# Two small matmuls of zeros in every 64th iteration of a three-layer convolution kernel

## The chip, the cores and the metric

The kernel runs on one core of a Trainium2 chip. The metric is the device time of one execution in microseconds (us). Of three runs of the kernel before, the median is 2720.43 us, the lowest 2719.11 and the highest 2721.21.

## The reference

The input `x` has the shape (4, 32, 32, 16): four batches, 32 x 32 pixels, 16 channels. Three layers of one form follow each other, and a fourth of another form. Cut to what matters:

```python
# layers 0, 1, 2, with x group-normalised first; the result is added to x
first   = einsum('ijpq,bpqc->bijc', M, x)
shifted = conv(x, G)                       # 3x3, 'SAME', for every output pixel (i,j) its own kernel
diff    = relu(x[:, :, :, None, None, :] - shifted)
second  = einsum('ijpq,bpqijc->bijc', W, diff)
x       = x + first - second
# layer 3: a rational 2-d filter, by Fourier transforms
```

The weight of the work is `second`: for each of 1024 output pixels (i,j) there is a 3x3 convolution of the whole image with kernels of its own, a relu, and a weighted sum over all 1024 input pixels.

## The kernel before

**The main loop.** One iteration takes one block `blk` (eight output pixels by 16 channels: 128 output partitions) and one batch `b`. There are 3 layers x 128 blocks x 4 batches = 1536 iterations. The list `order` holds them, and `now["at"]` is the number of the present one. Within an iteration TensorE (PE) fills a pair of PSUM banks `pt` [128, 2, 512] with x minus the convolution, and VectorE (DVE) reduces it with one instruction, L764: the minimum with 0, times the weight tile `w`, summed along the row.

**Two halves of the rows.** The contraction is only 64 long. So nearly every matmul uses 64 of the array's 128 rows: it is issued twice, first for partitions 0 to 63 (below: the upper half) into bank 0 of the pair, then for partitions 64 to 127 (the lower half) into bank 1. In the trace such an instruction has the tile form `64*128`: 64 rows by 128 columns. The two halves hold different data and write different banks, so nothing in the program ties one to the other.

**What an iteration issues.** The first 24 iterations go through `direct` (L699). All the others, 1512, go through `shared_products` and `own_products`:

- `shared_products(i + 1)`, L718: 3 matmuls for each half, 256 columns, in float32r (one pass), for the *next* iteration; ScalarE (ACT) then copies the result to the other half of the columns (L727).
- `own_products(i)`, L749: for each half two float32 matmuls of 256 columns, each of which the hardware does in two passes, so 4 passes; then two float32r matmuls of 512 columns.

So each half executes 9 weight loads and 9 matmul passes an iteration: 3 at L718, 4 at L749 with the tile `f`, and 2 at L749 with the tiles `n` and `g`. ACT clears part of a pair ahead of time (L681), and `prepare` gives out the four pairs in turn.

**What sets the order.** The order is written by hand (`manual_schedule`); the rest of the work is cut into generators that `step()` advances once an iteration: loads of `w`, `f` and `g`, GpSimd's preparation of taps, group norm (matmuls at L167 and L174, with `avg_r` as weights and zeros or statistics as moving data), the first term (`first_term`, L495, three times: 16 float32 matmuls of the form `128*64`, all 128 rows by 64 columns, in two passes each), and at the end layer 3 (L887, L927, L1067).

**Names in the change.** `avg_r` is a float32r constant [128, 128], `nought_r` is a [128, 2] tile of zeros, and `pt` is the pair that `own_products` accumulates into.

Of the kernel before, what the change touches and what calls it, by code (L numbers as in the profile page):

```python
# [15 lines left out]
P = 128  # L16
# [23 lines left out]
def conv_stack_kernel(ctx, tc, x, M, W, raw_f, first_g, F, E, h0, coef, cst, dft, idp, idq, out):  # L40
    nc = tc.nc
# [17 lines left out]
    def pair_psum(stays_full=False):  # L59
        slot = banks[0] % 4  # L60
        banks[0] += 1
        if not stays_full:
            full[slot] = False
        return ps.tile([P, 2, 512], F32, tag=f"pt{slot}", name="pt")
# [19 lines left out]
    avg_r = const.tile([P, P], F32R, name="avg_r")  # L84
# [4 lines left out]
    nought_r = const.tile([P, 2], F32R, name="nought_r")  # L89
# [14 lines left out]
    start = [[range(layer * NBLK + lo, layer * NBLK + hi) for lo, hi in spans[layer]] for layer in range(3)]  # L104
# [20 lines left out]
    now = {"at": 0}  # L125
# [470 lines left out]
    def taps_of(u, blk, half, dys, slot=1):  # L596
        rows = slice(64 * half, 64 * half + 64)
        if u < 3:
            return first_gt[u][rows, bass.ts(blk % GC, P)]
        v, blk = divmod(blk % GC, 2)  # L600
        return gt[uses[u][0]][rows, dys[half], v, slot, bass.ts(blk, P)]
# [7 lines left out]
    for q in qs:  # L609
        load = max(0, done[-2] + 5, ready[q] - 20)  # L610
        at = load, max(ready[q], done[-1] + 1, load + (6 if q else 3))
# [51 lines left out]
    def prepare(i, rearm=False):  # L663

        if i in pts or i >= len(order):
            return
        slot = banks[0] % 4
        if is_shared(i) and not full[slot] and not rearm and is_shared(now["at"]) and i == now["at"] + 2:
            return
        pts[i] = pt = pair_psum(True)  # L670
        if is_shared(i):
            if not full[slot]:
                blk, b, _ = order[now["at"]]
                ni = ims[blk // NBLK, b][1].rearrange("p y k m -> p (y k m)")
                for half in range(2):
                    rows = slice(64 * half, 64 * half + 64)
                    nc.tensor.matmul(
                        pt[:, half], lhsT=avg_r[rows], rhs=ni[rows, :512], start=True, stop=True
                    )
            here = by_pixel(pt)[:, :, 0]  # L680
            nc.scalar.copy(here, nought.unsqueeze(2).to_broadcast(list(here.shape)))  # L681
        full[slot] = True
# [4 lines left out]
    def of_half(pt, half, k):  # L687
        return pt[:, half].rearrange("p (l k x) -> p l k x", k=2, x=64)[:, :, k]
# [40 lines left out]
    def own_products(u, blk, b, pt):  # L729


        f = fours[uses[u][0]]
        at = bass.ts(blk % GC, P)
        fi, ni = ims[blk // NBLK, b]
        products = [lambda half, rows, k=k: (of_half(pt, half, k), f[rows, k, at], fi[rows, :, k]) for k in range(2)]
        for dys in ((0, 2), (2, 0)):
            products.append(
                lambda half, rows, dys=dys: (
                    pt[:, half],
                    taps_of(u, blk, half, dys),  # L740
                    ni[rows, dys[half] : dys[half] + 4, :2].rearrange("p l k m -> p l (k m)"),
                )
            )
        for n, operands in enumerate(products):
            if n == 2:
                prepare(now["at"] + 2, True)
            for half in range(2):
                to, w, rhs = operands(half, slice(64 * half, 64 * half + 64))
                nc.tensor.matmul(to, lhsT=w, rhs=rhs, start=False, stop=n == 3, skip_group_check=True)  # L749
# [434 lines left out]
    pt = pair_psum()  # L1184
# [175 lines left out]
```

## Time and profile before

| | value |
|---|---|
| median of 3 runs | 2720.43 us |
| the profiled execution's own time | 2729.58 us |
| its span, first to last instruction | 2727.8 us |
| PE busy | 2695.6 us (99%) |
| DVE busy | 1944.3 us (71%) |
| ACT busy | 1777.8 us (65%) |
| GpSimd busy | 845.6 us (31%) |
| mean granted TensorE clock | 0.997 |
| DMA | 652.93 MB, 239 GB/s |

The profiled execution is 9.2 us slower than the median of the runs, and 1.8 us of it lie around the span. "Busy" counts the time from an instruction's recorded start to its modelled end; matmuls overlap, so a busy PE may still lose time between two of them. A weight load (PEld) of the next matmul runs beside the present matmul. In this trace it begins about 2 ns after the present matmul's columns begin to stream, so that the starts of the weight loads tell when each pass really began.

### The profile page before, as it was taken

The page shows a single profiled execution, that of the slowest core. Times are in us where ns is not written, and L with a number is a line of the kernel's source. Part 1 is how long each engine was busy: PE and PEld are TensorE (multiplying, and loading weights), DVE is VectorE, ACT ScalarE, POOL GpSimd, SP SyncE. Part 2 cuts the span into 40 slices and gives each one's busy share as a digit, 9 for nine tenths or more (in the row PEclk, how much of TensorE's full clock was granted, in tenths as well). Part 3 has the DMA queues.
Part 4 walks back from the last instruction along what each step waited for, and adds up shares of the span by engine and source line. Part 5 has one row for each costly group of instructions (what it writes and reads, how often), then busy time and mean ns, then how long its engine had stood idle before and what let it go on. Part 6 is the DMA issues. An engine that isn't in the chain of part 4 may idle for free.

```text
span 2727.8 us, 69513 instructions
## 1 busy us (share of the span) xinstructions
PE 2695.6 (99%) x28402; PEld 2525.1 (93%) x28402; DVE 1944.3 (71%) x3246; ACT 1777.8 (65%) x3114; POOL 845.6 (31%) x1164
## 2 busy tenths in 40 slices
PE   7999999999999999999999999999999999999999
PEld 4899988888888899999999999989999999999995
DVE  6676876777777777677777777777767777777773
ACT  2566666666666676666666666666666666666661
POOL 5534354422312342322222221234332322232011
PEclk9999999999999999999999999999999999999999
DMA  8896567576664987565566657497866756676525
GB/s 298 300 343 235 185 229 273 203 264 221 254 257 182 315 258 292 211 244 225 223 231 239 246 219 282 179 326 240 316 210 225 265 218 254 228 249 241 224 84 84
DMA packets 134703, 652.93 MB, mean 239 GB/s; under 512 B 16992, under 2 KB 27376, under 8 KB 95344
## 3 DMA queue, kind: packets, MB, share of 16 engines
q1 hardware_dynamic: 85472, 475.99, 47.2%
q0 software_dynamic: 48480, 171.85, 19.6%
q8 instruction: 223, 3.65, 0.6%
q14 instruction: 96, 0.79, 0.1%
q10 hardware_dynamic: 432, 0.66, 0.1%
HBM read 488.81 MB, written 159.61 MB: 238 GB/s over the span
## 4 chain that ended last, share of the span: by engine, by line
PE 84%; DMA 1%; DVE 0%; POOL 0%; ACT 0%; issue 0%; SPq 0%; DVEq 0%; POOLq 0%
PE pt L749 67%; PE pt L718 14%; PE pt L1067 2%; DMA n<-img 1%; PE pt L495 1%; DMA g<-gd 0%; DMA img<-ye 0%; DVE junk L764 0%; ACT pt L681 0%; PE pt L887 0%; POOL ys L414 0%; POOL ys L421 0%; PE pt L167 0%; SPq L461 0%; PE pt L927 0%
## 5 line engine op out<-in xcount | busy, mean ns | idle before, releaser
L764 DVE SCALAR_TENSOR_TENSOR junk<-pt,w 128x1024 f32<-128x1024 f32 x1536 | 1881.0, 1225 | 736.0 <-PE pt L749 693.7
L749 PE MATMUL pt<-f,f 64*128 64x256 f32 x12096 | 1692.5, 377 | 0.0
L749 PE MATMUL pt<-n,g 64*128 64x512 f32 x6048 | 1354.5, 483 | 0.0
L749 PEld LDWEIGHTS pt<-f,f 64*128 64x128 f32 x12096 | 1212.3, 186 | 24.3
L681 ACT COPY pt<-nought_r 128x512 f32<-128x512 f32 x1512 | 888.7, 588 | 497.7 <-DVE junk L764 495.2
L727 ACT COPY pt<-pt 128x512 f32<-128x512 f32 x1512 | 860.7, 569 | 292.5 <-PE pt L718 291.7
L718 PEld LDWEIGHTS pt<-n,g 64*128 64x128 f32 x9072 | 919.2, 185 | 74.4 <-ACT pt L681 23.4
L718 PE MATMUL pt<-n,g 64*128 64x256 f32 x9072 | 920.8, 279 | 20.5 <-ACT pt L681 13.7
L749 PEld LDWEIGHTS pt<-n,g 64*128 64x128 f32 x6048 | 728.5, 187 | 22.6
L527 POOL TENSOR_TENSOR f<-f,cs 128x512 f32<-128x512 f32 x103 | 131.8, 1279 | 1170.0 <-DMA f<-in_F_dram 993.6
L566 POOL TENSOR_TENSOR raw<-raw 96x256 f32<-96x256 f32 x192 | 140.1, 729 | 7.7
L527 POOL TENSOR_TENSOR raw<-raw,cs 96x256 f32<-96x256 f32 x96 | 70.3, 732 | 215.2 <-DMA raw<-in_E_dram 215.0
L764 DVE DVE_READ_ACCUMULATOR junk<-pt,w 128x1 f32 x1536 | 128.0, 83 | 0.0
L572 POOL TENSOR_TENSOR raw<-raw,hi 96x512 fp32r<-96x512 f32 x96 | 122.9, 1281 | 7.0
L570 POOL CAST hi<-raw 96x512 fp32r<-96x512 f32 x96 | 58.3, 607 | 37.3 <-DMA gd<-hi 32.1
L576 POOL DMA_DIRECT2D gd<-hi x96 | 66.2, 690 | 0.0
L576 POOL DMA_DIRECT2D gd<-raw x96 | 65.1, 678 | 3.5 <-issue 3.5
L511 POOL DMA_DIRECT2D fd<-ft x48 | 25.0, 530 | 87.9 <-ACT ft L503 87.9
L699 PE MATMUL pt<-first_f,f 64*128 64x512 f32 x192 | 48.3, 621 | 0.0
L414 POOL TENSOR_TENSOR ys<-y 128x64 f32<-128x64 f32 x36 | 9.5, 292 | 99.3 <-DVE y L385 99.2
L699 PEld LDWEIGHTS pt<-first_f,f 64*128 64x128 f32 x192 | 19.7, 198 | 18.9 <-issue 12.0
L461 POOL DMA_DIRECT2D n<-img x48 | 25.0, 525 | 35.9 <-DMA img<-ye 20.4
(147 smaller groups left out, 407.5 us busy)
## 6 DMA issues: line engine op xcount, KB each, us to landing
w<-in_W_dram SPq DMA_DIRECT2D x199, 1024.0 KB, 11.5
g<-gd SPq DMA_DIRECT2D x100, 1536.0 KB, 10.2
gd<-hi POOLq DMA_DIRECT2D x96, 768.0 KB, 7.5
gd<-raw POOLq DMA_DIRECT2D x96, 768.0 KB, 9.1
f<-in_F_dram SPq DMA_DIRECT2D x103, 512.0 KB, 3.6
raw<-in_E_dram SPq DMA_DIRECT2D x96, 288.0 KB, 12.7
mt<-in_M_dram SPq DMA_DIRECT2D x12, 512.0 KB, 13.5
w<-in_M_dram SPq DMA_DIRECT2D x12, 512.0 KB, 17.1
```

The costliest lines, as they stand in the source:

```text
L527: engine.tensor_tensor(v, v, m.unsqueeze(1).to_broadcast([v.shape[0], v.shape[1], C]), ALU.subtract)
L566: nc.gpsimd.tensor_tensor(raw[:, 0], raw[:, 0], raw[:, k], ALU.add)
L570: nc.gpsimd.tensor_copy(hi, both)
L572: nc.gpsimd.tensor_tensor(lo, both, hi.bitcast(F32), ALU.subtract)
L576: nc.gpsimd.dma_start(out=gd[q % len(gd)][:, k].rearrange("a c n -> c a n"), in_=whole.unsqueeze(1).to_broadcast([96, 4, 4 * P]),)
L681: nc.scalar.copy(here, nought.unsqueeze(2).to_broadcast(list(here.shape)))
L699: nc.tensor.matmul(pt[:, half], lhsT=taps_of(u, blk, half, (0, 2)) if k == 2 else f[rows, k, at], rhs=t[rows], start=k == 0, stop=k == 2,)
L718: nc.tensor.matmul(of_half(pt, half, 0), lhsT=taps_of(u, blk, half, (dy, dy), 0), rhs=ni[rows, dy : dy + 4, 2], start=False, stop=dy == 2, ...
L727: nc.scalar.copy(v[:, :, 1], v[:, :, 0])
L749: nc.tensor.matmul(to, lhsT=w, rhs=rhs, start=False, stop=n == 3, skip_group_check=True)
L764: nc.vector.scalar_tensor_tensor(junk, pt.rearrange("p h m -> p (h m)"), 0.0, wts[w_at[i]][:, blk % 2, :], ALU.min, ALU.mult, accum_out=ac ...
L1067: nc.tensor.matmul(rows.rearrange("n (j r) -> n j r", j=C)[:, :, 8 * cc :], lhsT=y(cc).rearrange("p q b -> p (q b)"), rhs=ts[k][q][:, :, : ...
```

## The change

In `own_products`, in every iteration whose number leaves 8 when divided by 64, two matmuls are put ahead of the iteration's own ones. Their moving data are zeros, 16 columns wide, so they add 0 to what stands in `pt`. The first uses all 128 rows and adds to bank 0 of the pair, the second uses the lower half of the rows and adds to bank 1. Iteration 8 goes through `direct`, which has no such matmuls; so there are 23 places, iterations 72, 136, ..., 1480, and 46 matmuls. In the program's order of instructions PE has these 46 more, each time after the L718 matmuls of the next iteration and before the L749 matmuls of the present one; the order on DVE, ACT, GpSimd and SyncE is the same as before. After the change, what was L749 is L759, and L764 is L774.

```diff
         fi, ni = ims[blk // NBLK, b]
+        if now["at"] % 64 == 8:
+            for rows, h in ((slice(0, P), 0), (slice(64, P), 1)):
+                nc.tensor.matmul(
+                    pt[:, h, :16],
+                    lhsT=avg_r[rows],
+                    rhs=nought_r[rows].unsqueeze(1).to_broadcast([rows.stop - rows.start, 8, 2]),
+                    start=False,
+                    stop=False,
+                    skip_group_check=True,
+                )
         products = [lambda half, rows, k=k: (of_half(pt, half, k), f[rows, k, at], fi[rows, :, k]) for k in range(2)]
```

## The prediction

> **What bounds the kernel.** I read the page first. PE is busy for 99% of the span, and the chain of work that ended last is PE for 84% of it, by the two lines of the main loop:
>
> ```profile
> PE 2695.6 (99%) x28402; PEld 2525.1 (93%) x28402; DVE 1944.3 (71%) x3246; ACT 1777.8 (65%) x3114; POOL 845.6 (31%) x1164
> PE pt L749 67%; PE pt L718 14%; PE pt L1067 2%; DMA n<-img 1%; PE pt L495 1%; DMA g<-gd 0%; DMA img<-ye 0%; DVE junk L764 0%; ACT pt L681 0%; PE pt L887 0%; POOL ys L414 0%; POOL ys L421 0%; PE pt L167 0%; SPq L461 0%; PE pt L927 0%
> L764 DVE SCALAR_TENSOR_TENSOR junk<-pt,w 128x1024 f32<-128x1024 f32 x1536 | 1881.0, 1225 | 736.0 <-PE pt L749 693.7
> ```
>
> DVE waits 694 us for PE. An iteration costs DVE 1225 + 83 ns and ACT 588 + 569 ns, less than PE's 1.67 to 1.69 us: what PE loses is lost to the kernel, and no cover hides it.
>
> Next I read DVE's timeline. L764 ends each iteration, so its starts are the kernel's pulse. Two stretches (start, duration, what; idle before):
>
> ```profile
> 1949.70 1.22 DVE L764 SCALAR_TENSOR_TENSOR junk<-pt,w 128x1024 f32<-128x1024 f32 x1 [0.44 <-PE pt L749]
> ...
> 1956.39 1.23 DVE L764 SCALAR_TENSOR_TENSOR junk<-pt,w 128x1024 f32<-128x1024 f32 x1 [0.44 <-PE pt L749]
> ```
>
> ```profile
> 1449.30 1.22 DVE L764 SCALAR_TENSOR_TENSOR junk<-pt,w 128x1024 f32<-128x1024 f32 x1 [0.45 <-PE pt L749]
> ...
> 1456.05 1.23 DVE L764 SCALAR_TENSOR_TENSOR junk<-pt,w 128x1024 f32<-128x1024 f32 x1 [0.45 <-PE pt L749]
> ```
>
> Each pair is four iterations apart: 6.69 and 6.75 us. Over long stretches there are exactly two periods: 1673.3 and 1686.7 ns. Of the 1535 distances between ends of L764, 241 are the short one, 1141 the long one, 153 irregular. It isn't the clock; the table by stretches has 1.00 (the number ahead of the DMA share) in two slow stretches and a fast one (the third):
>
> ```profile
> 500.00:833.00 333.00, 333.00 (x3558) 294.31 (x3554) 243.59 (x395) 228.54 (x395) 92.22 (x113) 1.00 0.67 246
> 1154.00:1720.00 566.00, 566.00 (x6047) 566.00 (x6044) 413.49 (x671) 388.72 (x672) 147.49 (x179) 1.00 0.65 242
> 1837.00:1999.00 162.00, 162.00 (x1749) 155.64 (x1746) 119.96 (x199) 112.39 (x195) 51.06 (x67) 1.00 0.77 265
> ```
>
> Following the weight loads of one half at a time shows that each half of the rows has a period of its own, 1673.3 or 1686.7 ns, and keeps it until something stops PE. The slow pattern is 4 to 5 ns longer at several passes (from the last L718 pass to the first `f` pass 120 instead of 115 ns, then 220 instead of 215). Four combinations occur:
>
> - both halves fast: iteration 1673.3 (1837 to 1999 us; the lag between the halves stays at 23 ns);
> - both slow: 1686.7 (489 to 872 us; lag 3 ns);
> - one fast, one slow: the fast one runs ahead by 13.4 ns an iteration up to 120 ns, and is then held. The iteration is the slow half's, 1686.7.
>
> So the kernel is fast only while both halves are. Which combination holds changes only at a restart, where PE had stood still or done other work. After the three L495 blocks (205, 1123, 2000 us) it was the same each time: upper half fast, lower half slow. After restarts from a semaphore it looks random, both fast in about a third.
>
> **The change, part by part.** It removes nothing. It adds 23 x 2 matmuls, no DMA and nothing on another queue. The wait for ACT's copy (L727) moves from the first L749 weight load to the added one; behind it stands all of PE, as before, and the wait is already over in steady state. DVE and ACT then wait for PE as they do now.
>
> *Cost.* The first added matmul takes the array from two 64-row tiles to one of 128 rows, the second back. The nearest rows are the L495 blocks, 128 rows by 64 columns:
>
> ```profile
> 206.85 0.19 PEld L749 LDWEIGHTS pt<-n,g 64*128 64x128 f32 x1
> 207.40 0.20 PEld L495 LDWEIGHTS pt<-mt,yt 128*64 128x64 f32 x4 [0.36 <-DVE junk L764]
> ```
>
> ```profile
> 2007.48 0.14 PEld L495 LDWEIGHTS pt<-w,yt 128*64 128x64 f32 x2 [0.29 <-issue]
> 2008.43 0.42 PEld L718 LDWEIGHTS pt<-n,g 64*128 64x128 f32 x6 [0.81 <-issue]
> ```
>
> In the first, the last 64-row matmul begins at 207.075 and streams 213 ns (512 columns; a 512-column pass in a run is that long), to 207.288; the weight load of the new form comes 109 ns later instead of beside it, and takes 54 ns. On the way back, 94 ns pass after the last column, then a load of 107 ns. The iteration with the first block took 8894 ns in the lower half; less 1673 for itself and 16 x 428.5 for the block, 365 ns are left for both changes of form. The new weights have 128 columns, not 64: +54 ns; 16 columns stream in 7. The lower half's own small matmul costs what a 16-column one costs at L174, 110 ns, from its weight load at 874.196 to that of the next at 874.304: it is its weight load. Sum: 365 + 54 + 7 = 426 ns in the upper half, 536 in the lower.
>
> If the array did not have to empty for such a change of rows alone (every change in the trace alters the columns too), the cost would be two small matmuls in line: 220 ns. The bounds are 0.22 and 0.53 us. I take 0.43, two thirds of the way up, since the L495 rows, nearest in rows used, stand at the upper end. A gain from the matmuls as such is excluded: they compute nothing that another pass needs. Two of the 23 fall where PE waits for group norm (iterations 520 and 1032), and cost nothing. Cost: 21 x 0.43 = 9.0 us (4.6 to 12.2, the latter for 23).
>
> The Trainium skill, "TensorEngine Tiling (Array Packing)", section "Key Properties", says that changing the tiling mode drains TensorE. The gaps of 109 and 94 ns agree for a change of rows and columns; no run here shows rows alone. By that rule the sum is 12.2 us, without it 4.6.
>
> *Gain.* After the two matmuls both halves start afresh from one instant, without a wait, in the same way each time; the lower half comes some 110 ns behind. Left alone, a restart from 128 rows gave "upper fast, lower slow" three times of three; here the lower half does one matmul more before it goes on. If that puts both into the fast pattern, they stay so until the next restart. Counting from each place to the next restart, about 905 of the 1141 slow iterations come under it; some 235 lie between a restart and the next place. Gain: 905 x 13.4 ns = 12.1 us.
>
> *Sum:* 9.0 - 12.1 = -3.1 us, so the profiled execution's 2729.6 becomes 2726.5, and the median, by the same difference, 2717.3. That which a measurement here can tell from no change is 0.2%, 5.4 us.
>
> **Rivals.**
>
> *Never both fast (slower).* If the start after the two matmuls leaves either half slow, as the start after L495 does, nothing is won, and because the start is alike each time this would happen at all 23. The places now fast after them, some 200 iterations, are lost: 200 x 13.4 ns = 2.7 us. With 9.0 to 12.2 for the matmuls: +11.7 to +14.9, 2732 to 2735. For it: L495. Against: the added matmul acts on just the half that was slow there. It decides from the point where fewer than 9.0 us / 13.4 ns = 670 iterations become fast.
>
> *By chance (slower).* If the pattern falls out as at restarts from semaphores, a third is fast instead of 241 of 1382: 0.16 x 1382 x 13.4 ns = 3.0 us won, 9.0 paid: +6.0, 2726. Against it: there is no wait of random length in the new start.
>
> *Both fast and cheap (faster).* With 0.22 us a place and the gain of 12.1: -7.0 to -7.5, 2713; with all 1141 iterations won, 15.3 - 5.1 = -10, 2710. The forecast passes into it where a place costs less than (12.1 - 5.4) / 23 = 0.29 us.
>
> *The change does nothing.* Excluded: the order of the built program has 46 more PE instructions, none elsewhere. A queue cannot end up late: DMA engines are busy for 63 to 77% of the stretches above, and only PE's times move.
>
> **The numbers.** Both halves fast: 0.52, of which 0.33 at a cost low enough (or a gain high enough) for over 0.2% and 0.19 within 0.2%; its own range is 2711 to 2723, the forecast 2717.3. Never both fast: 0.34. By chance: 0.14. These two are slower by over 0.2%: 0.48. The range reaches from the cheap end, 2711, to 2733.5 in the first rival; about a tenth is left out on either side.
>
> **What would show it.** Right: the starts of L774 stand 1673.3 ns apart from 72 on wherever no restart has come since the last place, above all from 505 to 833 us and from 1154 to 1720; the weight load of the 128-row matmul stands some 100 ns behind the last column of L718, and the iteration of a place is 0.2 to 0.53 us longer. Wrong: 1686.7 ns remains after the places, or the two alternate; a lag that grows by 13.4 ns an iteration would say which half is slow. A place that costs 0.8 us or more, or a third period, would overturn the sum.

## The result, and the profile after

The changed kernel took 2730.73 us (median of 6 runs, 2727.83 to 2733.94), the kernel before 2720.82 (6 runs, 2719.11 to 2722.40): a ratio of 1.0034, 95% interval 1.0024 to 1.0044. It is slower by 0.34%; the forecast was 0.1% faster.

Yet the profile of the changed kernel (own time 2727.8 us) shows nearly all that the forecast described. DVE's timeline in the stretch that was shown of before (start, duration, what; idle before):

```profile
1449.71 1.23 DVE L774 SCALAR_TENSOR_TENSOR junk<-pt,w 128x1024 f32<-128x1024 f32 x1 [0.44 <-PE pt L759]
...
1456.41 1.23 DVE L774 SCALAR_TENSOR_TENSOR junk<-pt,w 128x1024 f32<-128x1024 f32 x1 [0.44 <-PE pt L759]
```

Four iterations now take 6.70 us, not 6.75. Counted over the whole trace, 1063 iterations run at 1673 ns and 309 at 1687 (before: 241 and 1141). Where both halves are fast behind a place, the lower stands 103 to 110 ns behind the upper, for 64 iterations on end, as the working said.

The timeline around one place (iteration 264):

```profile
504.97 1.23 DVE L774 SCALAR_TENSOR_TENSOR junk<-pt,w 128x1024 f32<-128x1024 f32 x1 [0.44 <-PE pt L759]
...
507.15 1.23 DVE L774 SCALAR_TENSOR_TENSOR junk<-pt,w 128x1024 f32<-128x1024 f32 x1 [0.95 <-PE pt L759]
508.82 1.22 DVE L774 SCALAR_TENSOR_TENSOR junk<-pt,w 128x1024 f32<-128x1024 f32 x1 [0.44 <-PE pt L759]
```

The iteration of the place takes 2.18 us, the next one 1.67 again: a place costs 0.51 us. The two matmuls in the groups of PEld, and the weight loads at one place (iteration 712):

```profile
L737 PEld LDWEIGHTS pt<-nought_r,avg_r 128*128 128x128 f32 x23 | 4.3, 186 | 3.1
L737 PEld LDWEIGHTS pt<-nought_r,avg_r 64*128 64x128 f32 x23 | 4.2, 183 | 0.5
```

```profile
1274.83 0.39 PEld L737 LDWEIGHTS pt<-nought_r,avg_r 128*128 128x128 f32 x2
1275.04 0.40 PEld L759 LDWEIGHTS pt<-f,f 64*128 64x128 f32 x4
```

The load with 128 rows (1274.830 in the trace) stands about 98 ns behind the last L718 column; 207 ns later, at 1275.037, the lower half's load begins (107 for the load, 7 for 16 columns, 93 of standstill); and 108 to 111 ns behind it, at 1275.145 and 1275.148, two more loads begin, one of them that half's first `f` load. So the array does empty when only the rows change, as the Trainium skill ("TensorEngine Tiling (Array Packing)", "Key Properties") has it for any change of mode; before, no row showed rows alone.

Between the two profiles, 309 slow iterations instead of 1141 are worth 11.1 us, and 22 places of 0.51 cost 11.3 (the 23rd is hidden, as shown further down). By that sum the two executions should be equal to 0.2 us; they took 2729.6 and 2727.8. What then made the timed ones differ by 9.9?

### The profile page after: what moved, and what is told of

The parts are those of the page before. It is cut to its first block, busy times and chain, and to the rows that moved or that the text cites. A ratio compares the mean times of both kernels' runs of the same rounds, so it can differ in the third digit from the quotient of the medians.

```text
span 2726.0 us, 69601 instructions
## 1 busy us (share of the span) xinstructions
PE 2693.5 (99%) x28448; PEld 2555.7 (94%) x28448; DVE 1944.4 (71%) x3246; ACT 1778.6 (65%) x3114; POOL 845.5 (31%) x1164
## 4 chain that ended last, share of the span: by engine, by line
PE 84%; DMA 1%; DVE 0%; POOL 0%; ACT 0%; issue 0%; SPq 0%; DVEq 0%; POOLq 0%
PE pt L759 64%; PE pt L718 17%; PE pt L1077 2%; DMA n<-img 1%; PE pt L495 1%; DMA g<-gd 0%; DVE junk L774 0%; DMA img<-ye 0%; PE pt L737 0%; ACT pt L681 0%; PE pt L897 0%; POOL ys L414 0%; POOL ys L421 0%; PE pt L167 0%; PE pt L937 0%
## 5 line engine op out<-in xcount | busy, mean ns | idle before, releaser
L774 DVE SCALAR_TENSOR_TENSOR junk<-pt,w 128x1024 f32<-128x1024 f32 x1536 | 1880.9, 1225 | 733.8 <-PE pt L759 690.4
L759 PE MATMUL pt<-f,f 64*128 64x256 f32 x12096 | 1721.8, 377 | 0.0
L759 PE MATMUL pt<-n,g 64*128 64x512 f32 x6048 | 1388.5, 482 | 0.0
L759 PEld LDWEIGHTS pt<-f,f 64*128 64x128 f32 x12096 | 1255.7, 186 | 13.9
L718 PEld LDWEIGHTS pt<-n,g 64*128 64x128 f32 x9072 | 950.4, 185 | 57.7 <-ACT pt L681 23.5
L718 PE MATMUL pt<-n,g 64*128 64x256 f32 x9072 | 948.4, 278 | 19.4 <-ACT pt L681 13.7
L759 PEld LDWEIGHTS pt<-n,g 64*128 64x128 f32 x6048 | 760.6, 187 | 13.2
L774 DVE DVE_READ_ACCUMULATOR junk<-pt,w 128x1 f32 x1536 | 127.9, 83 | 0.0
```

The lines of the kernel that those rows point to most:

```text
L718: nc.tensor.matmul(of_half(pt, half, 0), lhsT=taps_of(u, blk, half, (dy, dy), 0), rhs=ni[rows, dy : dy + 4, 2], start=False, stop=dy == 2, ...
L774: nc.vector.scalar_tensor_tensor(junk, pt.rearrange("p h m -> p (h m)"), 0.0, wts[w_at[i]][:, blk % 2, :], ALU.min, ALU.mult, accum_out=ac ...
```

## The experiments

Each run has a label (e1 to e12), given in its heading. The ratio given with each is to the kernel before in the same comparison. Worked back from the first profile, an execution of the kernel before takes 2714.3 us plus 13.4 ns for each slow iteration.

### The kernel before, run again (e1, e9, e10, e11)

Edit: none. Four more profiles, and runs of the kernel before beside every other kernel.

> The kernel before, unchanged. Two theories for the 9.2 us by which its first profiled execution (2729.6 us) lay above its timed ones (2720.4 to 2720.8). Mix: how many iterations run at the slow period differs from one execution to the next; the first profile had 1141 of them and was an unlucky one. Worked back from it, an execution takes 2729.6 - 1141 x 13.4 ns = 2714.3 us plus 13.4 ns for each slow iteration, so a time of 2720.5 means about 460 slow ones. The profile of this run should then obey that sum, whatever its time: 2720 with some 430, 2730 with some 1150. Overhead: the mix is about the same in every execution, and that profile was slow for another reason. Then this run shows again 1000 or more slow iterations beside a time of 2720.

> The kernel before, once more with a profile, for a further pair of time and number of slow iterations. Mix theory: the time is 2713.5 us (worked back from the profiles so far: 2729.6 less 1141 x 13.4 ns is 2714.3, 2726.1 less 929 x 13.4 is 2713.7) plus 13.4 ns for each slow iteration, within 2 us; and the number differs from 1141 and 929. Overhead theory: no relation.

> As the run before it: 2713.5 us plus 13.4 ns for each slow iteration, within 2 us, and another number of slow iterations.

> As the two runs before it: 2713.5 us plus 13.4 ns for each slow iteration, within 2 us, and another number of slow iterations. The behaviour after the L495 blocks (upper half fast and lower slow three times in the first profile, once both fast in the second) should differ again.

Measured:

| profile of the kernel before | its own time | slow iterations | time less 13.4 ns each |
|---|---|---|---|
| the first | 2729.6 us | 1141 | 2714.3 |
| e1 | 2726.1 | 929 | 2713.7 |
| e9 | 2722.0 | 559 | 2714.5 |
| e10 | 2725.0 | 781 | 2714.5 |
| e11 | 2728.3 | 920 | 2716.0 |

The last column varies by 2.3 us, the time by 7.6. So the mix theory holds: the number of slow iterations is drawn anew in every execution, and sets most of its time. The sum is good to 2 or 3 us, no better: e11 lies 2.5 us above its expectation, and with the places of the changed kernels taken off too, what is left of the profiles below spreads from 2711 to 2716 us. Timed beside e1 to e4, 29 runs of the kernel before spread from 2715.07 to 2729.91 us, median 2725.39; beside e5 to e8, 31 runs, 2716.78 to 2729.79, median 2723.94; beside e12, 12 runs, 2716.84 to 2728.03, median 2722.95. The 11 runs of e1, the same kernel once more, have the median 2726.76 (2722.28 to 2731.74), a ratio of 1.0007 (0.9997 to 1.0016) to the 29: that much the comparison of a kernel with itself can show. The six runs of the first comparison, 2719.1 to 2722.4, were low and narrow. Only 16 of the 72 runs of the three later comparisons fall into that band, so that six of six did is hardly chance alone; why is not known.

Two long stretches behind the second and third L495 block decide most of it, 367 and 374 iterations, 5 us each. In the table by stretches (DVE's busy time and number of instructions in 566 and 569 us; a faster pulse puts more into the same time) the first profile has both slow, e9 both fast, e10 the first fast and e11 the second (in this order):

```profile
1154.00:1720.00 566.00, 413.49 (x671) 1.00 0.65 242
2031.00:2600.00 569.00, 416.09 (x675) 1.00 0.66 240
```

```profile
1154.00:1720.00 566.00, 416.69 (x677) 1.00 0.65 244
2031.00:2600.00 569.00, 419.01 (x681) 1.00 0.66 243
```

```profile
1154.00:1720.00 566.00, 417.02 (x678) 1.00 0.66 244
2031.00:2600.00 569.00, 415.63 (x675) 1.00 0.66 240
```

```profile
1154.00:1720.00 566.00, 413.79 (x671) 1.00 0.65 242
2031.00:2600.00 569.00, 419.06 (x681) 1.00 0.66 242
```

The start behind L495, which looked fixed in the first profile (three of three), is drawn too: both halves came out fast behind 6 of the 15 blocks of these five profiles.

### The 128-row matmul alone (e2)

```diff
-            for rows, h in ((slice(0, P), 0), (slice(64, P), 1)):
+            for rows, h in ((slice(0, P), 0),):
```

> Only the first added matmul, over all 128 rows, 23 times. It should cost what the upper half pays in the changed kernel, about 0.40 us a place (iteration of 2.08 us instead of 1.67), 9.2 us in all. Lower half needed: the restart is then like that after L495, upper half fast and lower slow, from each place on: some 1350 to 1450 slow iterations, 2714.3 + 19 + 9.2 = 2742 us. Change of form enough: both halves fast after each place, some 250 slow iterations as in the changed kernel, 2714.3 + 3.5 + 9.2 = 2727 us.

Measured: 2725.60 us (12 runs), ratio 1.0006 (0.9997 to 1.0016). The profile has 249 slow iterations; from every place on, both halves are fast until the next restart, 2 to 23 ns apart. A place's iteration takes 2081 to 2094 ns; with the one behind it (2088 + 1665 where all was fast before) a place costs 0.407 us. So the 128-row matmul is enough, and the second isn't needed. What in it does the setting isn't separated: the change of rows, the standstill of 93 to 98 ns on either side of it, or the common start of both halves. No run stops PE at this point without a change of rows. In DVE's timeline behind the place 648 the pulse settles to 1.67 us within two iterations (the first line is that of the place; the short second instruction of each L774 is left out):

```profile
1168.47 1.23 DVE L774 SCALAR_TENSOR_TENSOR junk<-pt,w 128x1024 f32<-128x1024 f32 x1 [0.85 <-PE pt L759]
1170.16 1.22 DVE L774 SCALAR_TENSOR_TENSOR junk<-pt,w 128x1024 f32<-128x1024 f32 x1 [0.45 <-PE pt L759]
1171.84 1.23 DVE L774 SCALAR_TENSOR_TENSOR junk<-pt,w 128x1024 f32<-128x1024 f32 x1 [0.45 <-PE pt L759]
1173.51 1.23 DVE L774 SCALAR_TENSOR_TENSOR junk<-pt,w 128x1024 f32<-128x1024 f32 x1 [0.44 <-PE pt L759]
1175.19 1.22 DVE L774 SCALAR_TENSOR_TENSOR junk<-pt,w 128x1024 f32<-128x1024 f32 x1 [0.44 <-PE pt L759]
```

### The lower half's matmul alone (e3)

```diff
-            for rows, h in ((slice(0, P), 0), (slice(64, P), 1)):
+            for rows, h in ((slice(64, P), 1),):
```

> Only the second added matmul, over the lower half, 23 times; the form of the tiles never changes. It should cost one 16-column matmul in the lower half, 0.11 us a place, 2.5 us in all, and the lower half should stand 110 ns behind from the first place on. If the pattern of a half is set only where PE starts afresh: the mix stays that of the kernel before, 2720.5 + 2.5 = 2723 us. If the one more matmul in the lower half is what sets it to the fast pattern: about 300 slow iterations, 2714.3 + 4 + 2.5 = 2721 us, and the profile shows 1673 ns after each place.

Measured: 2722.00 us (12 runs), ratio 0.9992 (0.9982 to 1.0002): the time tells neither theory apart. The profile does: 1105 slow iterations, and the 63 behind 264, behind 328 and behind 392 all slow, right through the places; 584 and 1096, which find both halves fast, leave them fast. A matmul in one half without a change of form moves that half by 0.11 us (places of 1790 to 1796 ns where the lower half sets the pulse) and leaves the pattern.

This profile also tells which half is which, since its matmul falls on the lower half alone. Followed through the trace (the lag is taken at each half's last L718 pass), the lower half stands 3 ns behind the upper before 264, then 110, 216 and 323 ns behind 264, 328 and 392. Behind the second and third L495 block it is *ahead*, by 140 ns: the place 712 cuts its lead to 40, nine iterations later it is 140 again, and the pulse shows nothing. The L774 before the place's and the place's own, at 264 and at 712:

```profile
502.32 1.23 DVE L774 SCALAR_TENSOR_TENSOR junk<-pt,w 128x1024 f32<-128x1024 f32 x1 [0.45 <-PE pt L759]
...
504.11 1.23 DVE L774 SCALAR_TENSOR_TENSOR junk<-pt,w 128x1024 f32<-128x1024 f32 x1 [0.56 <-PE pt L759]
```

```profile
1271.46 1.23 DVE L774 SCALAR_TENSOR_TENSOR junk<-pt,w 128x1024 f32<-128x1024 f32 x1 [0.45 <-PE pt L759]
...
1273.15 1.23 DVE L774 SCALAR_TENSOR_TENSOR junk<-pt,w 128x1024 f32<-128x1024 f32 x1 [0.45 <-PE pt L759]
```

That is 1.79 us and 1.69. So behind L495 the lower half is the fast one and the upper, slow, sets the pulse. The same reading of the first profile has it so behind all three of its L495 blocks; the prediction and some of the expectations name the halves the other way round.

### Twice as many places (e4)

```diff
-        if now["at"] % 64 == 8:
+        if now["at"] % 32 == 8:
```

> Both matmuls every 32nd iteration: 47 places instead of 23. Priced at 0.513 us a place (2187 ns for the iteration of a place less 1673, from the profile of the changed kernel), the 24 more cost 12.3 us; slow stretches are ended sooner, which wins 1 to 2 us: 2730.7 + 12.3 - 1.5 = 2741 to 2742 us. If instead a place costs little and the 10 us of the change come from something else, about 2731.

Measured: 2739.81 us (6 runs), ratio 1.0060 (1.0046 to 1.0073), 1 to 2 us below what 0.51 us a place lets expect; a place's iteration takes 2176 to 2202 ns in the profile, as in the changed kernel. Slow stretches did not get fewer: 308 slow iterations against 309. That the 10 us of the change come from the places fits; within the 2 or 3 us of the sum, nothing else is needed.

### The changed kernel again (e5)

Edit: none to the changed kernel.

> The changed kernel again, beside the kernel before on one chip. Its cost is 23 x 0.513 = 11.8 us and it leaves some 300 slow iterations; the kernel before has between 150 and 1150 of them from one execution to the next. Mix theory: the difference depends on how the executions of the kernel before fell; against the 2725.4 us of the 29 runs of the last comparison it is 2730.5, ratio 1.002, not 1.0034; and its own runs spread less than those before (6 us against 15), since a pattern now lives for 64 iterations at most. If the ratio is a property of the kernels alone: 1.0034 again.

Measured: 2728.78 us (12 runs, 2726.09 to 2730.89) against 2723.94 (31 runs), ratio 1.0018 (1.0008 to 1.0028). The spread is 5 us against 13. This is what the mix theory asks for: the changed kernel's mix is nearly set, the kernel before's is drawn. The ratio alone doesn't decide, since its interval and that of the first comparison (1.0024 to 1.0044) overlap a little; in both, the changed kernel is the slower one. That the changed kernel itself came out 2 us lower than the first time isn't explained. The profile has 399 slow iterations, and again the 63 behind the place 648 and the 63 behind 1160 are slow.

### The 128-row matmul at five places behind the restarts (e6)

```diff
-        if now["at"] % 64 == 8:
-            for rows, h in ((slice(0, P), 0), (slice(64, P), 1)):
+        if now["at"] in (258, 530, 629, 1042, 1141):
+            for rows, h in ((slice(0, P), 0),):
```

> The 128-row matmul alone, at five places, each just behind a stretch of restarts: iterations 258, 530, 629, 1042, 1141. Cost 5 x 0.407 = 2.0 us (2080 ns less 1673, from the profile of the kernel with that matmul alone). If each of them sets both halves to the fast pattern until the next restart, 226 + 98 + 367 + 98 + 374 iterations are fast and some 170 slow ones remain: 2714.3 + 2.0 + 2.3 = 2719 us in every execution, 6 us below the kernel before's 2725.4, with a small spread. If setting needs several tries, or holds only by chance, 2722 to 2726 with a wide spread.

Measured: 2715.05 us (10 runs, 2712.21 to 2718.05), ratio 0.9968 (0.9956 to 0.9980): faster than both kernels, and 4 us below the expectation, which the sum doesn't explain. The profile (2717.0 us) has 145 slow iterations; all five stretches behind the places are fast to their end, in the table by stretches both long ones:

```profile
1154.00:1720.00 566.00, 417.06 (x677) 1.00 0.66 243
2031.00:2600.00 569.00, 419.11 (x680) 1.00 0.66 240
```

### Both matmuls at the same five places (e7)

```diff
-        if now["at"] % 64 == 8:
+        if now["at"] in (258, 530, 629, 1042, 1141):
```

> The same five places with both matmuls of the change. In the profile of the changed kernel the places 648 and 1160, the first behind an L495 block with the upper half ahead, left the iterations slow (63 each), and the 128-row matmul alone did not. Second matmul spoils it there: iterations 629 to 995 and 1141 to 1514 stay slow, 2714.3 + 5 x 0.513 + (170 + 741) x 13.4 ns = 2729 us. Chance: all five work, 2719.5 us.

Measured: 2717.24 us (12 runs), ratio 0.9977 (0.9968 to 0.9987), 143 slow iterations. Right behind L495, both matmuls set both halves fast, so the 2729 us fall. But the theory that the second matmul spoils the start isn't tested by this: one iteration behind the block the halves stand 2 ns apart, while at 648 and 1160 the lower had run 140 ns ahead. There both matmuls left the iterations slow in every profile that has them (that of the changed kernel, e4, e5), and the 128-row matmul alone did not (e2). The second matmul costs 0.1 us a place more, and leaves the lag at 103 to 110 ns.

### The 128-row matmul ahead of L718 (e8)

```diff
+        if i % 64 == 8 and is_shared(i):
+            nc.tensor.matmul(pts[i][:, 0, :16], lhsT=avg_r, rhs=..., start=False, stop=False, ...)
         shared_products(i + 1)
```

> The 128-row matmul alone, every 64th iteration as in the change, but ahead of the L718 matmuls instead of behind them: the new start then begins with a one-pass float32r matmul as the start after L495 does, not with the two-pass float32 ones. First pass decides: the start is like that after L495, one half fast and one slow in most places; 900 to 1400 slow iterations, 2714.3 + 9.4 + 12 to 19 = 2736 to 2742 us. Change of rows decides wherever it stands: some 250 slow iterations, 2726 us.

Measured: 2735.36 us (10 runs), ratio 1.0041 (1.0027 to 1.0055). The profile (2739.5 us) has 1071 slow iterations; both long stretches are slow (671 and 675 instructions in the first profile, which has no places in them):

```profile
1154.00:1720.00 566.00, 411.71 (x668) 1.00 0.65 240
2031.00:2600.00 569.00, 414.06 (x673) 1.00 0.66 240
```

A place costs the same (2081 to 2092 ns), but it sets nothing. Of the 23 places, 18 have an undisturbed stretch behind them, and at all 18 the iterations go on as they came: 15 times slow (three times with both halves slow, twelve with the upper slow and the lower ahead), three times fast (72, 584, 1096). Only the lag is drawn in, to 3 or 7 ns. So the time and the number of slow iterations are near those of the first theory, but not for its reason, and the second falls: a change of rows by itself isn't enough. It sets the pattern where it stands between the L718 and the `f` passes. Whether what runs before it there matters, or what follows, isn't shown; the move changed both.

### Both matmuls in the opposite order (e12)

```diff
-            for rows, h in ((slice(0, P), 0), (slice(64, P), 1)):
+            for rows, h in ((slice(64, P), 1), (slice(0, P), 0)):
```

> Both matmuls, the lower half's first and the 128-row one last. The lower half's costs 0.11 us in its half, the 128-row one 0.407: 23 x 0.517 = 11.9 us, as much as the change. Last matmul sets the pattern: then this behaves like the 128-row matmul alone, all places fast, 648 and 1160 too, lag of 3 to 10 ns, and 120 fewer slow iterations than the changed kernel, 1.7 us less: about 2727. Order makes no difference: 2728.8 to 2730.7 us, 648 and 1160 stay slow.

Measured: 2732.50 us (7 runs), ratio 1.0035 (1.0022 to 1.0047). Neither theory: 648 and 1160 are fast, as for the 128-row matmul alone, but elsewhere fast and slow stretches take turns, 690 slow iterations in all. Behind 264 four iterations take 6.75 us, behind 328 three take 5.02:

```profile
508.57 1.23 DVE L774 SCALAR_TENSOR_TENSOR junk<-pt,w 128x1024 f32<-128x1024 f32 x1 [0.45 <-PE pt L759]
...
515.32 1.23 DVE L774 SCALAR_TENSOR_TENSOR junk<-pt,w 128x1024 f32<-128x1024 f32 x1 [0.45 <-PE pt L759]
```

```profile
618.59 1.22 DVE L774 SCALAR_TENSOR_TENSOR junk<-pt,w 128x1024 f32<-128x1024 f32 x1 [0.44 <-PE pt L759]
...
623.61 1.22 DVE L774 SCALAR_TENSOR_TENSOR junk<-pt,w 128x1024 f32<-128x1024 f32 x1 [0.44 <-PE pt L759]
```

In the trace a place that finds both halves fast, with the upper 3 to 10 ns ahead, leaves the lower slow (264, 392, 776, 904, 1288, 1416), and one that finds the upper ahead by 400 to 465 leaves both fast (72, 328, 840, 968, 1352, 1480). So the outcome hangs on how the halves stood when the place came, not only on the matmul that comes last. Counted the same way, at all places with an undisturbed stretch behind them, it does so in each kernel in its own way:

| places | lower half ahead before | level or upper ahead before |
|---|---|---|
| both matmuls (the changed kernel, e4, e5) | 8, by 4 to 140 ns: all left slow | 66, by 3 to 465 ns: all left fast |
| the 128-row one alone (e2) | 5, by 10 to 140 ns: all left fast | 13, by 2 to 429 ns: all left fast |
| opposite order (e12) | 6, by 4 to 140 ns: all left fast | by 3 to 10 ns, 6: left slow; by 400 to 465 ns, 6: left fast |
| ahead of L718 (e8) | 12, by 140 ns: slow, as they came | 6, by 2 to 103 ns: three slow, three fast, as they came |

The table was drawn up from the profiles afterwards; no run was made to test it.

## Why the prediction was wrong

- **The two periods, their cause in the halves, and that PE has no cover.** Right, in every profile.
- **"If that puts both into the fast pattern, they stay so until the next restart".** Right in both profiles of the changed kernel at every place with an undisturbed stretch behind it, but for 648 and 1160. The reason given for it was wrong: not the lower half's further matmul but the 128-row one, ahead of `f`, sets them (e2 against e3). At 648 and 1160 the further matmul did harm.
- **"Upper half fast, lower half slow" behind L495.** The wrong way round: the lower was fast there and the upper slow (e3). So the added matmul did not act "on just the half that was slow there". Nor is the half ahead always held at 120 ns: the lower is held at 140 (taken at the last L718 pass), but behind the places 648 and 1160 the upper ran ahead to 465.
- **The gain, 905 x 13.4 ns = 12.1 us. This is the step that failed.** Between the two profiled executions it is there, 11.1 us. But it was counted from one execution with 1141 slow iterations and then taken off a median that, by its time, held far fewer. The text put the 9.2 us between that execution and the median down as a mere offset ("by the same difference"). By the sum of the table, 2720.8 us means some 480 slow iterations (e9, profiled at 2722.0 us, had 559; the timed runs themselves have no profile); 309 to 399 remain after, so the gain against the timed runs was 1 to 2 us. That makes 10.6 of the 13.4 us between the forecast 2717.3 and the measured 2730.7.
- **The cost, 0.43 us a place.** Mis-sized, and the smaller part of the miss, 2.3 us: 0.513 measured (2187 ns less 1673). The step-by-step sum in the text, 0.536, was nearer; taking two thirds of the way to a lower bound without a row of its own moved it off. And not two places were free but one: 136 (2751 ns, 2749 without it), while 520 and 1032, named as free, took 2748 and 2746 ns against 2237 and 2238 before. 22 x 0.513 = 11.3 us, not 9.0.
- **The sum again:** 11.3 - 1.5 = +9.8 us; measured +9.9. That it fits to 0.1 us is luck: against the 31 runs beside e5, whose median means some 710 slow iterations, 11.3 - 4.2 = +7; measured +4.8.
- **The rivals.** "Never both fast" falls: the result lies near its time, by another road. "By chance" falls for the changed kernel, where the outcome followed how the halves stood, but fits the kernel before, whose mix is drawn. "Cheap" falls: the array empties.
- **Two readings.** The two lines of the main loop make 81% of the chain of work (67 + 14), not 84. And the two times that the lower half's matmul is read from are 108 ns apart, not 110; e3 moved that half by 106 to 107. Neither changes the forecast.

What stays open: what in the hardware keeps a half at one period or the other; why the lag before a place decides what both matmuls leave behind; why the six runs of the kernel before were so low and close together; and the 2 us between the two sets of runs of the changed kernel.

## What to carry to other kernels

Where one kernel's profiled time and its timed median differ by as much as the effect that is looked for, find out what differs before a gain is counted from the profile; a second profile of the unchanged kernel would have told here. A reset that costs half a microsecond belongs behind the events that spoil the state, not on a clock: five places won 0.32% where 23 lost 0.18 to 0.34%. And where a cost has been summed from rows, keep the sum.

## What the runs showed of the hardware

Two halves of PE's rows, fed the same kind of work, each run at one of two periods (1673.3 or 1686.7 ns for nine passes, at a granted clock of 1.00 in both) and keep it for hundreds of iterations. The lower half got at most 140 ns ahead of the upper, the upper 465 ns ahead of the lower. A change from 64-row tiles to a 128-row one and back costs 0.407 us with 16 columns in it. Between the float32r passes of L718 and the float32 passes of L749 it set both halves to the shorter period at all 18 places that could show it (e2); ahead of the L718 passes it changed neither half's period at any of 18 (e8). A single small matmul in one half costs that half 0.11 us and sets nothing.
